# Two attention blocks: transposed exponentials moved within SBUF, value products 512 queries wide, shares of a step rearranged

## The chip, the cores and the metric

The kernel runs on one core of one Trainium2 chip. The metric is the device time of one execution in microseconds. The kernel before takes 3504.99 us, the median of three runs (3502.89 to 3509.22).

## The reference

Two layers follow each other on `x` of shape (4, 32, 32, 768) in fp32. Each is `x + attention(group_norm(x))`, with 32 groups of 24 channels and 12 heads of 64.

```
qkv = x @ Wqkv                       # second layer: + bias
scores = scale * q k^T + rel_h[..., :, None] + rel_w[..., None, :]
out = softmax(scores) @ v
x = x + out @ Wproj + bproj
```

`rel_h` and `rel_w` are products of each query with the table rows of its distance along height and width. An image has 1024 positions, so a head's scores are 1024 x 1024. The second layer has `scale` applied twice.

## The kernel before, in words

**Tiling.** There are 8 images (2 layers x 4), 6 pairs of heads in each, so 48 pairs `g`. A pair has 8 blocks of 128 queries, `n` = 0 to 7. One turn of the main loop (L566) is a unit (g, n), 384 in all. Channels lie on the partitions, and the two heads of a pair on partitions 0 to 63 and 64 to 127.

**What a unit does.** The order of all engines is written out by hand (`manual_schedule`, L566 to L625): an engine carries its instructions out in the order of the program, and one that waits holds those behind it. In unit (g, n):

- `biases` (L312) for the unit after the next: GpSimd adds the two position terms into `sc`.
- `scores` (L326) for the next unit: TensorE multiplies q and k into PSUM (tile `s`), VectorE subtracts from the biases and takes the row's extreme (L342), ScalarE exponentiates and sums (L346).
- `turn` (L358) for this unit: VectorE transposes the divided exponentials in 32 x 32 blocks into `tb` (L370).
- `divide` (L351) for the next unit: VectorE inverts the sums, GpSimd multiplies (L356).
- a share of the other matmuls, taken by `take` from the list `todo`.
- at n = 2 and n = 6 `weigh` (L386): the product of the transposed exponentials and v.

**Transposing through DRAM.** A 32 x 32 block transpose leaves the blocks themselves in place. Every second `turn` therefore writes `tb` of each head to DRAM (`td`, L373: 1 MB) and, one or two units later, reads it back as `pt` in 2 KB runs with the key's position spread over all partitions (`read_back`, L378). Both are issued by SyncE. A quarter is two blocks of queries; `weigh` takes two quarters, each with 256 query columns, and 8 key chunks for either head. The two heads use different columns of the TensorE array (128 x 64), while `scores`, the projections and `positions` split its rows (64 x 128) and the output projection uses the whole array.

**The shares.** One step of a generator in `todo` is a share: two half-array matmuls of 512 columns (`project_in` L202, tile `pj`), four of 256 columns (`project_values` L237, tile `pv`), or one full-array matmul of 512 columns (`project_out` L467, tile `o`). At n = 0 `todo` gets the q and k projections of the next pair (24 shares), half of two pairs' values (12) and a part of the output projection (12, in pairs that have one). The list `shares` (L570) says how many of the 48 go into each n; `first` (L608) says how many come ahead of `turn`, which orders VectorE's evictions against its transposes.

**Lists of later work.** Closures in `early` run at the start of the next unit, those in `later` one unit after that, those in `behind` and `behind2` after `scores` one or two units on. The q projection queues `positions` (L269, tile `tp`: products with the distance tables, written to DRAM by ScalarE's queue as `tdr`), and its second half queues `diagonals` (L295), 16 small DMAs on SyncE which read `rel` back for the next pair. SyncE's queue also carries the weights, the images, residuals and results.

**Buffers.** `pt` has two buffers for each head (8 KB a partition each), `tb` three (8 KB), `sc` six. PSUM holds two `s` tiles of two banks, and two tiles of two banks for all else.

Of the kernel before, what the change touches and what calls it, by code (L numbers as in the profile page):

```python
# [31 lines left out]
FP = mybir.dt.float32  # L32
# [4 lines left out]
P = 128  # L37
B, HW, C = 4, 32, 768
S = HW * HW
NH, D = 12, 64  # L40
NC = C // P
NT = S // P
# [3 lines left out]
HALF = 512  # L46
LAYERS = 2
NP = NH // 2
# [6 lines left out]
def attention_blocks(ctx: ExitStack, tc: tile.TileContext, a: dict, out: bass.AP):  # L55
    nc = tc.nc
# [8 lines left out]
    vpool = ctx.enter_context(tc.tile_pool(name="v", bufs=3))  # L65
    scpool = ctx.enter_context(tc.tile_pool(name="sc", bufs=6))
    tmppool = ctx.enter_context(tc.tile_pool(name="tmp", bufs=1))
    tbpool = ctx.enter_context(tc.tile_pool(name="tb", bufs=3))
    ptpool = ctx.enter_context(tc.tile_pool(name="pt", bufs=2))
    relpool = ctx.enter_context(tc.tile_pool(name="rel", bufs=2))  # L70
    iopool = ctx.enter_context(tc.tile_pool(name="io", bufs=4))
    small = ctx.enter_context(tc.tile_pool(name="small", bufs=4))
# [11 lines left out]
    NPAIR = NI * NP  # L84
# [117 lines left out]
    def project_in(g, which, i):  # L202

        im, pair = divmod(g, NP)
        xn, w = xn_of[im], w_of[g, which]
        cols = slice(i * HALF, (i + 1) * HALF)
        if i == 0:
            tag = "qk"[which]
            qk_of[g, which] = qkpool.tile([P, S], FP, tag=tag, name=f"{tag}_{g}")
        t = ps_m.tile([P, 2, HALF], FP, tag="m", name=f"pj_{g}_{which}_{i}")  # L210
        for c in range(NC):
            for a in range(2):
                rows = slice(a * D, (a + 1) * D)
                nc.tensor.matmul(  # L214
                    t[:, a, :], lhsT=w[rows, c, :], rhs=xn[c][rows, cols],
                    start=(c == 0), stop=(c == NC - 1),
                )
            if c < NC - 1:
                yield True
        to, t = qk_of[g, which], [t[:, a, :] for a in range(2)]  # L220
        if which == 1:
            to = to.rearrange("p (a m) -> p a m", a=4)[:, :, i * P : (i + 1) * P]
            t = [x.rearrange("p (m a) -> p a m", a=4) for x in t]
        else:
            to = to[:, cols]
        if images[im][0] == 0:
            nc.scalar.copy(to, t[0])  # L227
        else:
            nc.scalar.activation(to, t[0], AF.Identity, bias=bqkv[:, which, pair : pair + 1])
        nc.vector.tensor_tensor(to, t[1], to, ALU.add)  # L230
        if which == 0:
            (later if g else mid).append(lambda: positions(g, i))
        if i == 1 and g + 1 < NPAIR:
            later.append(lambda: load_w(g + 1, which))
        yield True
# [121 lines left out]

    def turn(g, n):  # L358

        quarter, j = divmod(n, 2)
        for h in range(2):
            if j == 0:
                tb_of[h] = tbpool.tile([P, HW, 2, HW], FP, tag="tb", name=f"tb_{g}_{n}_{h}")
            tb = tb_of[h]
            nc.vector.transpose(tb[:, :, j, :], sc_of[g, n, h])  # L370
            if j == 1:
                td = dram2.tile([P, S * 2], FP, tag=f"td{h}", name=f"td_{g}_{n}_{h}")
                nc.sync.dma_start(out=td, in_=tb.rearrange("p k n i -> p (k n i)"))  # L373
                (behind if quarter % 2 else behind2).append(
                    lambda queue=None, h=h, td=td: read_back(g, quarter, h, td, queue)
                )

    def read_back(g, quarter, h, td, queue=None):  # L378
        pt = ptpool.tile([P, 4, NT, 2 * HW], FP, tag=f"pt{h}", name=f"pt_{g}_{quarter}_{h}")
        pt_of[g, quarter, h] = pt  # L380
        (queue or nc.sync).dma_start(
            out=pt.rearrange("p r k t -> p r (k t)"),
            in_=td.rearrange("(r j) (a t) -> (j a) r t", r=4, a=4),
        )

    def weigh(g, quarters):  # L386

        if quarters[0] == 0:
            attn_of[g] = apool.tile([P, S], FP, tag="attn", name=f"attn_{g}")
        n = len(quarters)
        av = ps_m.tile([P, S], FP, tag="m", name=f"av_{g}_{quarters[0]}")[:, : n * 2 * P]
        for at, quarter in enumerate(quarters):
            for k in range(NT):
                for h in range(2):
                    rows = slice(h * D, (h + 1) * D)
                    nc.tensor.matmul(  # L399
                        av[rows, at * 2 * P : (at + 1) * 2 * P], lhsT=v_of[g][:, k, rows],  # L400
                        rhs=pt_of[g, quarter, h][:, :, k, :], start=(k == 0), stop=(k == NT - 1),
                    )
        at = quarters[0] * 2 * P
        to = attn_of[g][:, at : at + n * 2 * P].rearrange("p (q n r i) -> p q r n i", q=n, n=2, r=4)
        av = av.rearrange("p (q r n i) -> p q r n i", q=n, n=2, r=4)
        im, pair = divmod(g, NP)
        if images[im][0] == 0:
            nc.vector.tensor_copy(to, av)
        else:
            for q in range(n):  # L410
                nc.vector.tensor_scalar(to[:, q], av[:, q], bqkv[:, 2, pair : pair + 1], None, ALU.add)

    def cuts(im):
        return [0, NC // 2, NC] if im + 1 < NI else [0, NC // 2, NC - 1, NC]
# [86 lines left out]

    early, mid, later, behind, behind2 = [], [], [], [], []

    def run(todo):
        while todo:  # L510
            todo.pop(0)()
# [30 lines left out]
    with tc.manual_schedule(engines=ENGINES):  # L542
# [23 lines left out]
        for at, (g, n) in enumerate(units):  # L566
            im, pair = divmod(g, NP)
            end = im + 1 == NI
            if n == 0:
                shares = [6, 6, 0, 6, 12, 6, 0, 12]  # L570
                ins = (todo if at == 0 else []) + prepare(g + 1)
                if pair < 3:
                    if at == 0:
                        shares = [12, 6, 0, 6, 12, 6, 0, 0]
                    todo = ins + (put_out(im - 1, 1, range(4 * pair, 4 * pair + 4)) if im else [])
                elif pair < NP - 1:
                    todo = ins + put_out(im, 0, range(4 * pair - 12, 4 * pair - 8))
                    if pair == 3 and not end:
                        stages, apply = norm(im + 1)
                else:  # L580
                    todo = ins + put_out(im, 0, range(8, 12))
                    if end:
                        fetch_last()
                        todo += put_out(im, 1, range(12)) + put_out(im, 2, range(0, 12, 2))
                        shares = [6, 6, 0, 6, 6, 2, 0, 4]
            if (pair, n) in loads and not end:
                load_x(im + 1, loads[pair, n])
            if im + 1 < B:
                if (pair, n) in loads0:
                    load_x(im + 1, loads0[pair, n], loads0[pair, n] + AHEAD)  # L590
                if pair < 3 and n in (1, 3, 5, 6):
                    c, i = divmod(4 * pair + n // 2, 2)
                    x = xn_of[im + 1][c % AHEAD][:, i * HALF : (i + 1) * HALF]
                    later.append(lambda c=c, i=i, x=x: stats(im + 1, (c + AHEAD) % NC, i, x))
            run(early)
            early, later = later, early
            if at + 2 < len(units):
                biases(*units[at + 2])
            if at + 1 < len(units):
                scores(*units[at + 1])  # L600
            run(behind)
            behind, behind2 = behind2, behind
            if pair == 3 and n in stages and not end:
                stages[n]()
            if pair == 4 and n in (2, 4, 6) and not end:
                apply(n // 2 - 1)
            share = shares[n]
            first = 3 if n == NT - 1 else 2 if end and pair == NP - 1 and n in (3, 4) else 0  # L608
            first = min(first, share)
            take(todo, first)  # L610
            share -= first
            turn(g, n)
            if at + 1 < len(units):
                divide(*units[at + 1])
            if pair == 4 and n == 7 and not end:
                for chunks in ((3, 4), (5,)):
                    take(todo, 3)
                    share -= 3
                    for c in chunks:
                        apply(c)  # L620
            take(todo, share)
            if n == 6:
                weigh(g, (0, 1))
            elif n == 2 and g:
                weigh(g - 1, (2, 3))  # L625
        for read in behind:
            read(nc.scalar)
        take(todo, 12)
        for quarter in (2, 3):
            weigh(NPAIR - 1, (quarter,))  # L630
        todo = put_out(NI - 1, 2, range(1, 12, 2))
        take(todo, len(todo))

# [54 lines left out]
```

## Time and profile before

| | before |
|---|---|
| median of three runs | 3504.99 us |
| span of the profiled execution | 3507.0 us |
| mean granted TensorE clock | 0.998 |
| idle of TensorE | 44.7 us, 25.7 of it at the start |
| DMA | 1084.54 MB, mean 309 GB/s |
| td<-tb, SyncE | x384, 1024 KB, 5.9 us to landing |
| pt<-td, SyncE | x382, 1024 KB, 7.6 us to landing |
| rel<-tdr, SyncE | x760, 32 KB, 2.3 us to landing |

The profile is of one execution, and of it the page gives the span alone. The chain of work that ended last is followed back from the last instruction; where it stays on one engine, that engine's own work sets the time. In its list in order of time a line has start, length, engine, tile, source line and the number of instructions. Idle time of an engine off the chain costs nothing.

### The profile page before, as it was taken

Reading aid. Unit: us, or ns where it says so; the run is one execution under the profiler, and the core shown is the slowest. Engines: PE = TensorE matmul, PEld = TensorE weight load, DVE = VectorE, ACT = ScalarE, POOL = GpSimd, SP = SyncE. Lnnn points to the kernel's source line nnn. Section 1 sums busy time; section 2 is a strip of 40 time slices with the busy share of each in tenths; the row PEclk is TensorE's granted clock in tenths of the full one; section 3 lists DMA queues with packets and bytes.
Section 4 is the critical chain, followed back from the end, with each engine's and each line's share of the span. In section 5 each row is a group of like instructions: output and inputs, shape, how many; then the busy total and the mean of one; then the engine's idle time right before and its main releaser. Section 6 shows DMA issues by size and latency. Waiting matters only on the chain.

```text
span 3507.0 us, 55102 instructions
## 1 busy us (share of the span) xinstructions
PE 3462.3 (99%) x21120; PEld 1921.4 (55%) x21120; DVE 2381.1 (68%) x3676; ACT 1227.5 (35%) x2040; POOL 2729.9 (78%) x1546
## 2 busy tenths in 40 slices
PE   6999999999999999999999999999999999999999
PEld 4555555555555555555555555555555555555554
DVE  4666767767677676767767667666666667666666
ACT  2334333333333333333333333333333333333331
POOL 3888887778777787788777788787787778787774
PEclk9999999999999999999999999999999999999999
DMA  4889989999899898898989989899889988898877
GB/s 137 312 308 311 332 293 337 319 316 326 304 329 323 313 316 313 312 324 305 326 305 326 320 292 332 311 331 306 300 327 324 321 298 316 319 322 295 311 275 281
DMA packets 624857, 1084.54 MB, mean 309 GB/s; under 512 B 247120, under 2 KB 310096, under 8 KB 575440
## 3 DMA queue, kind: packets, MB, share of 16 engines
q1 hardware_dynamic: 569008, 1028.29, 83.4%
q10 hardware_dynamic: 55584, 52.72, 4.4%
q8 instruction: 166, 2.72, 0.3%
q14 instruction: 99, 0.81, 0.1%
HBM read 580.59 MB, written 500.27 MB: 308 GB/s over the span
## 4 chain that ended last, share of the span: by engine, by line
PE 97%; DMA 2%; DVE 0%; SPq 0%; issue 0%; ACT 0%; POOL 0%; ACTq 0%; DVEq 0%
PE pj L214 28%; PE s L333 19%; PE av L399 19%; PE o L475 14%; PE pv L249 14%; PE tp L281 3%; DMA tdr<-t 1%; DMA pt<-td 1%; SPq L307 0%; DMA td<-tb 0%; DMA wo<-in_wo 0%; DMA xn<-in_x 0%; DVE st L152 0%; DMA rel<-tdr 0%; DMA per<-mv 0%
## 5 line engine op out<-in xcount | busy, mean ns | idle before, releaser
L319 POOL TENSOR_TENSOR sc<-rel 128x1024 f32<-128x1024 f32 x768 | 1890.4, 2485 | 38.2 <-DMA rel<-tdr 38.2
L356 POOL TENSOR_SCALAR sc<-sc,sm 128x1024 f32<-128x1024 f32 x768 | 855.1, 1127 | 686.1 <-DVE sm L353 669.2
L346 ACT ACTIVATE sc<-sc,sm 128x1024 f32<-128x1024 f32 x768 | 879.8, 1147 | 1370.9 <-DVE sm L342 1368.7
L342 DVE CUSTOM_DVE_ANT_0 sc<-s,sc 128x1024 f32<-128x1024 f32 x768 | 909.8, 1222 | 293.3 <-PE s L333 266.4
L214 PE MATMUL pj<-xn,w 64*128 64x512 f32 x4608 | 1033.5, 591 | 26.8 <-DVE xn L193 25.7
L370 DVE STREAM_TRANSPOSE tb<-sc 128x1024 f32<-128x1024 f32 x768 | 910.7, 1222 | 22.9 <-DMA td<-tb 20.5
L214 PEld LDWEIGHTS pj<-xn,w 64*128 64x128 f32 x4608 | 453.2, 188 | 568.6 <-issue 536.6
L333 PE MATMUL s<-k,q 64*128 64x512 f32 x3072 | 750.1, 598 | 7.0 <-DVE sm L342 6.9
L399 PE MATMUL av<-pt,v 128*64 128x256 f32 x6144 | 689.1, 382 | 6.1 <-DMA pt<-td 6.1
L399 PEld LDWEIGHTS av<-pt,v 128*64 128x64 f32 x6144 | 434.5, 137 | 289.8 <-ACT v L259 35.6
L249 PE MATMUL pv<-wv,xn 64*128 64x256 f32 x4608 | 515.7, 376 | 0.0
L249 PEld LDWEIGHTS pv<-wv,xn 64*128 64x128 f32 x4608 | 448.3, 187 | 90.8 <-issue 30.1
L475 PE MATMUL o<-attn,wo 128*128 128x512 f32 x1080 | 475.8, 597 | 0.2 <-DMA wo<-in_wo 0.2
L333 PEld LDWEIGHTS s<-k,q 64*128 64x128 f32 x3072 | 288.5, 187 | 299.5 <-issue 275.5
L475 PEld LDWEIGHTS o<-attn,wo 128*128 128x128 f32 x1080 | 201.4, 190 | 271.4 <-issue 260.9
L260 DVE TENSOR_TENSOR v<-pv,v 128x256 f32<-128x256 f32 x192 | 81.5, 425 | 277.6 <-ACT v L259 277.6
L259 ACT COPY v<-pv 128x256 f32<-128x256 f32 x192 | 71.5, 372 | 330.7 <-PE pv L249 282.9
L286 ACT COPY t<-tp 128x1024 f32<-128x1024 f32 x96 | 97.2, 1012 | 245.5 <-PE tp L281 148.5
L346 ACT ACTIVATION_READ_ACCUMULATOR sc<-sc,sm 128x1 f32 x768 | 143.6, 187 | 0.0
L230 DVE TENSOR_TENSOR q<-pj,q 128x512 f32<-128x512 f32 x96 | 66.4, 692 | 107.5 <-ACT q L227 56.0
L230 DVE TENSOR_TENSOR k<-pj,k 128x512 f32<-128x512 f32 x96 | 66.4, 692 | 95.5 <-ACT k L227 49.0
L281 PEld LDWEIGHTS tp<-tab,q 64*128 64x128 f32 x1536 | 100.0, 187 | 39.9 <-issue 39.6
(34 smaller groups left out, 787.6 us busy)
## 6 DMA issues: line engine op xcount, KB each, us to landing
td<-tb SPq DMA_DIRECT2D x384, 1024.0 KB, 5.9
pt<-td SPq DMA_DIRECT2D x382, 1024.0 KB, 7.6
tdr<-t ACTq DMA_DIRECT2D x96, 512.0 KB, 6.3
w<-in_wqk SPq DMA_DIRECT2D x96, 384.0 KB, 7.5
rel<-tdr SPq DMA_DIRECT2D x760, 32.0 KB, 2.3
part<-res SPq DMA_DIRECT2D x84, 256.0 KB, 5.5
res<-part SPq DMA_DIRECT2D x84, 256.0 KB, 9.1
wv<-in_wv SPq DMA_DIRECT2D x24, 768.0 KB, 8.7
```

The costliest lines, as they stand in the source:

```text
L214: nc.tensor.matmul(t[:, a, :], lhsT=w[rows, c, :], rhs=xn[c][rows, cols], start=(c == 0), stop=(c == NC - 1),)
L230: nc.vector.tensor_tensor(to, t[1], to, ALU.add)
L249: nc.tensor.matmul(t[:, a, k, :], lhsT=xn[c][rows, (2 * i + k) * P : (2 * i + k + 1) * P], rhs=w[rows, c, :], start=(c == 0), stop=(c == N ...
L281: nc.tensor.matmul(ps[:, h, j, :], lhsT=q[rows, at * P : (at + 1) * P], rhs=tabs[l][rows, :], start=True, stop=True,)
L319: nc.gpsimd.tensor_tensor(sc.rearrange("p (a k) (u l) -> p a (k u) l", a=4, l=8), rel[:, h, 0, n, :].unsqueeze(1).unsqueeze(3).to_broadcas ...
L333: nc.tensor.matmul(ps[h][:, cols], lhsT=q[rows, n * P : (n + 1) * P], rhs=k[rows, cols], start=True, stop=True,)
L342: nc.vector.tensor_tensor_reduce(out=sc, in0=ps[h], in1=sc, scale=-scale, scalar=BIG, op0=ALU.add, op1=ALU.min, accum_out=st[:, 0, h : h + 1],
L346: nc.scalar.activation(sc, sc, AF.Exp, bias=st[:, 0, h : h + 1], scale=-1.0, accum_out=st[:, 1, h : h + 1],)
L356: nc.gpsimd.tensor_scalar(sc, sc, st[:, 2, h : h + 1], 1.0, ALU.mult, ALU.mult)
L370: nc.vector.transpose(tb[:, :, j, :], sc_of[g, n, h])
L399: nc.tensor.matmul(av[rows, at * 2 * P : (at + 1) * 2 * P], lhsT=v_of[g][:, k, rows], rhs=pt_of[g, quarter, h][:, :, k, :], start=(k == 0) ...
L475: nc.tensor.matmul(t, lhsT=wo_of[im, o, c], rhs=attn_of[im * NP + c][:, cols], start=(c == c0), stop=(c == c1 - 1),)
```

## The change

The two heads of two blocks now share one tile `tb` of 16 KB a partition, with two buffers. When both blocks are in it, `move` issues 16 DMAs on SyncE from `tb` straight to `pt`, each from 32 partitions to every fourth of 128, in runs of 4 KB. `pt` holds four blocks of both heads (32 KB a partition) and has one buffer. `weigh` takes four blocks at once: 512 query columns a matmul, at n = 5 for the first half and at n = 1 of the next pair for the second. The list `behind2` goes; a move is issued in the unit after its second `turn`. The shares per n are rearranged, three of them precede `turn` at n = 6 as well as at n = 7, and `positions` of the first half of q runs one unit after its projection instead of two. After the last unit, all remaining shares come ahead of the last `weigh`. [...]

```diff
-    tbpool = ctx.enter_context(tc.tile_pool(name="tb", bufs=3))
-    ptpool = ctx.enter_context(tc.tile_pool(name="pt", bufs=2))
+    tbpool = ctx.enter_context(tc.tile_pool(name="tb", bufs=2))
+    ptpool = ctx.enter_context(tc.tile_pool(name="pt", bufs=1))
...
-            (later if g else mid).append(lambda: positions(g, i))
+            (mid if not g else later if i else early).append(lambda: positions(g, i))
...
     def turn(g, n):
-        quarter, j = divmod(n, 2)
+        b, j = divmod(n, 2)
+        if j == 0:
+            tb_of[b] = tbpool.tile([P, HW, 2, 2, HW], FP, tag="tb", name=f"tb_{g}_{b}")
+        tb = tb_of[b]
         for h in range(2):
...
-            nc.vector.transpose(tb[:, :, j, :], sc_of[g, n, h])
-            if j == 1:
-                td = dram2.tile([P, S * 2], FP, tag=f"td{h}", name=f"td_{g}_{n}_{h}")
-                nc.sync.dma_start(out=td, in_=tb.rearrange("p k n i -> p (k n i)"))
-                (behind if quarter % 2 else behind2).append(
-                    lambda queue=None, h=h, td=td: read_back(g, quarter, h, td, queue)
+            nc.vector.transpose(tb[:, :, h, j, :], sc_of[g, n, h])
+        if j == 1:
+            behind.append(lambda: move(g, b, tb))
+
+    def move(g, b, tb):
+        half, u = divmod(b, 2)
+        if u == 0:
+            pt_of[g, half] = ptpool.tile(
+                [P, 2, 4, NT * 4 * HW], FP, tag="pt", name=f"pt_{g}_{half}"
+            )
+        pt = pt_of[g, half].rearrange("(j a) u r x -> a j u r x", a=4)
+        src = tb.rearrange("p (a k) h n i -> p a (k h n i)", a=4)
+        for a in range(4):
+            for r in (0, 2, 1, 3):
+                nc.sync.dma_start(out=pt[a][:, u, r, :], in_=src[r * HW : (r + 1) * HW, a, :])
+
+    def weigh(g, half):
...
+        av = ps_m.tile([P, S], FP, tag="m", name=f"av_{g}_{half}")[:, :HALF]
+        pt = pt_of[g, half].rearrange("p u r (k h x) -> p (u r) k h x", k=NT, h=2)
+        for k in range(NT):
+            for h in range(2):
+                rows = slice(h * D, (h + 1) * D)
+                nc.tensor.matmul(
+                    av[rows, :], lhsT=v_of[g][:, k, rows], rhs=pt[:, :, k, h, :],
+                    start=(k == 0), stop=(k == NT - 1),
                 )
...
-                shares = [6, 6, 0, 6, 12, 6, 0, 12]
+                shares = [12, 0, 6, 6, 12, 0, 6, 6]
...
-                        shares = [12, 6, 0, 6, 12, 6, 0, 0]
+                        shares = [12, 6, 6, 6, 12, 0, 0, 0]
...
-                        shares = [6, 6, 0, 6, 6, 2, 0, 4]
+                        shares = [6, 0, 6, 5, 4, 0, 5, 2]
...
-            first = 3 if n == NT - 1 else 2 if end and pair == NP - 1 and n in (3, 4) else 0
+            first = 0 if n < 6 else 2 if end and pair == NP - 1 else 3
...
-            if n == 6:
-                weigh(g, (0, 1))
-            elif n == 2 and g:
-                weigh(g - 1, (2, 3))
-        for read in behind:
-            read(nc.scalar)
-        take(todo, 12)
-        for quarter in (2, 3):
-            weigh(NPAIR - 1, (quarter,))
+            if n == 5:
+                weigh(g, 0)
+            elif n == 1 and g:
+                weigh(g - 1, 1)
+        run(behind)
+        take(todo, len(todo) * NC)
+        weigh(NPAIR - 1, 1)
...
-    nc = bacc.Bacc("TRN2", target_bir_lowering=False, num_devices=1)
+    nc = bacc.Bacc("TRN2", target_bir_lowering=False, num_devices=1, dynamic_dma_scratch_size=1024)
```

More of the change, by code (lines that the diff above doesn't have):

```diff
@@ L358, in turn @@
     def turn(g, n):
-        quarter, j = divmod(n, 2)
+        b, j = divmod(n, 2)
+        if j == 0:
+            tb_of[b] = tbpool.tile([P, HW, 2, 2, HW], FP, tag="tb", name=f"tb_{g}_{b}")
+        tb = tb_of[b]
         for h in range(2):
-            if j == 0:
-                tb_of[h] = tbpool.tile([P, HW, 2, HW], FP, tag="tb", name=f"tb_{g}_{n}_{h}")
-            tb = tb_of[h]
-            nc.vector.transpose(tb[:, :, j, :], sc_of[g, n, h])
-            if j == 1:
-                td = dram2.tile([P, S * 2], FP, tag=f"td{h}", name=f"td_{g}_{n}_{h}")
-                nc.sync.dma_start(out=td, in_=tb.rearrange("p k n i -> p (k n i)"))
-                (behind if quarter % 2 else behind2).append(
-                    lambda queue=None, h=h, td=td: read_back(g, quarter, h, td, queue)
-                )
@@ L378, in read_back @@
[L378 to L405, printed above, removed]
@@ new lines, in weigh @@
+    def weigh(g, half):
+        if half == 0:
+            attn_of[g] = apool.tile([P, S], FP, tag="attn", name=f"attn_{g}")
+        av = ps_m.tile([P, S], FP, tag="m", name=f"av_{g}_{half}")[:, :HALF]
[6 more added lines that the diff above has]
+                    start=(k == 0), stop=(k == NT - 1),
+                )
+        to = attn_of[g][:, half * HALF : (half + 1) * HALF]
+        to = to.rearrange("p (q n r i) -> p q r n i", q=2, n=2, r=4)
+        av = av.rearrange("p (q r n i) -> p q r n i", q=2, n=2, r=4)
@@ L409, in weigh @@
         else:
-            for q in range(n):
+            for q in range(2):
                 nc.vector.tensor_scalar(to[:, q], av[:, q], bqkv[:, 2, pair : pair + 1], None, ALU.add)
@@ L501, in project_out @@
         yield True
-    early, mid, later, behind, behind2 = [], [], [], [], []
+    early, mid, later, behind = [], [], [], []
     def run(todo):
@@ L601, in attention_blocks @@
             run(behind)
-            behind, behind2 = behind2, behind
             if pair == 3 and n in stages and not end:
```

## The prediction

> **What bounds the kernel now.** I read the page's busy shares and its chain first, then the chain in order of time for one pair, then the groups of the DMA issues, and last SyncE's queue beside VectorE.
>
> ```profile
> PE 3462.3 (99%) x21120; PEld 1921.4 (55%) x21120; DVE 2381.1 (68%) x3676; ACT 1227.5 (35%) x2040; POOL 2729.9 (78%) x1546
> PE 97%; DMA 2%; DVE 0%; SPq 0%; issue 0%; ACT 0%; POOL 0%; ACTq 0%; DVEq 0%
> ```
>
> TensorE is busy 3462.3 of 3507.0 us and carries 97% of the chain; DMA carries 2%. Of the idle 44.7 us, 25.7 are the wait for the first normalised image. The page's DMA row stands at 8 to 9 tenths, yet between 210 and 3420 us TensorE is busy 3208.55 of 3210.00 us. So halving the bytes is worth nothing by itself there. Only what changes TensorE's own sequence, or makes it wait, moves the time. The sequence, from the chain in order of time (start, length, line, passes; each fp32 matmul of the program runs as two passes):
>
> ```profile
> 1532.92 1.72 PE s L333 x8
> 1534.64 7.06 PE av L399 x64
> 1541.69 1.92 PE s L333 x8
> 1543.61 10.50 PE o L475 x24
> 1554.11 1.92 PE s L333 x8
> 1556.03 5.15 PE pj L214 x24
> 1561.18 1.72 PE s L333 x8
> 1562.89 5.15 PE pj L214 x24
> 1568.04 0.89 PE tp L281 x16
> 1568.94 1.72 PE s L333 x8
> 1570.65 7.06 PE av L399 x64
> 1577.71 1.09 PE tp L281 x16
> ...
> 1615.31 10.50 PE o L475 x24
> ```
>
> A pair lasts 1615.31 - 1543.61 = 71.70 us. A 512-column pass on a half array takes 5.15 / 24 = 214.6 ns, so two side by side 429.2; twelve full-array passes elsewhere take 5.35 against 10.50 for 24, so one pass is (10.50 - 5.35) / 12 = 429.2 ns and the rest, 0.20 us, is paid once per group. Likewise `s` takes 1.72 after a row-split group and 1.92 after `o` or `av`; `tp` 0.89 and 1.09. Each visit to `o` therefore costs 0.20 on entry and 0.20 on leaving, 0.40 us, besides its passes.
>
> [...] Here 429.2 per side-by-side pair of 512 columns, and for `pv` at 256 columns 5.18 / 24 = 215.8; twice that less 429.2 is 2.4 ns. [...] No operation before shows an SBUF to SBUF transfer[...].
>
> **The change, part by part.**
>
> *Value products, 512 wide.* 6144 passes become 3072. Pass work: 64 x 215.8 / 2 = 6.91 us per weighing before (7.06 with its entry), 32 x 214.6 = 6.87 after. 0.04 x 96 weighings = 3.8 us gained. Bounds: 0 if the loss is per column, 5.5 if the 0.15 entry goes too. The 3072 weight loads removed (137 ns each, 421 us of PEld) lie beside running matmuls: in `av`, PEld is idle 290 us. Worth nothing.
>
> *Shares.* Of 48 shares per pair, 36 are projections and the last 12 the output projection. Before, [6, 6, 0, 6, 12, 6, 0, 12] leaves exactly the final 12 for n = 7: one visit to `o`. After, [12, 0, 6, 6, 12, 0, 6, 6] spends 36 by n = 4, so `o` runs in n = 6 and in n = 7, with unit 0's `s` of the next step between: s, o, s, o, s. One visit more per pair, 0.40 us. Pairs 3 to 46 have 12 such shares: 44 x 0.40 = 17.6 us lost. Bounds: 8.8 if only entry counts, 17.6 if both. I take 17.6, since both steps stand in the chain above. Visits to `av` stay two per pair, in n = 5 and n = 1 instead of 6 and 2. The last pair keeps its six visits.
>
> *DMAs.* Per pair 8 + 8 transfers of 1 MB go, 64 of 128 KB come. Issue and landing, from the answers by line:
>
> ```profile
> L373 SPq DMA_DIRECT2D td<-tb x384: 319/332/1607, 80.4 to 3474.9; - x192
> L307 SPq DMA_DIRECT2D rel<-tdr x760: 302/449/1812, 50.6 to 3389.6; - x190
> ```
>
> The three figures are the least, median and greatest ns on SyncE. 64 x 0.33 = 21 us of SyncE per pair replace 8 x 0.33 + 8 x 0.38 = 5.7; with the 16 `rel` DMAs (7.2) and some 10 us of others that is 40 of 72. SyncE is not full, so only its order matters. A move needs 16 x 0.33 = 5.3 us to issue and some 2 us for the last to land: 7.3 us. [...] I take 9.
>
> *Are the moves in time?* VectorE's transposes end 6.5 us after their unit's `s` starts (`s` at 1507.11, transposes 1511.26 to 1513.62). A unit of 6 shares lasts 1.72 + 5.15 = 6.87 us, so `turn` of n = 3 ends as unit 4 starts. Unit 4 has 12 shares (12.05 us), unit 5 only `s` (1.72) before `weigh`: 13.8 us of cover, less what stands ahead on SyncE. Ahead stand the 16 `rel` DMAs. `positions` of the second half now runs at n = 2 instead of 3; after TensorE's 0.9, ACT's 1.0 and the transfer's 6.3 median they can go at about the start of unit 3, take 7.2 to 10.7, and leave SyncE 1 to 4 us into unit 4. So 10 to 13 us remain for 9 needed. The other half: unit 0 has 12 shares, unit 1 `tp` and `s`, 14.9 us; ahead stand two `res` writes which wait for VectorE's eviction of the last `o` group, about 2 us in. 12.5 us remain. Both fit: cost 0. Without cover each microsecond late costs 48 us a half. Behind the waiting move stand only weight and image loads due units later.
>
> *One `pt` buffer, two `tb`.* The first move of a half waits for the weighing before it; `weigh` ends with unit 5 (or 1), the move follows in unit 6 (or 2) and is due 3 units later. Each `tb` is read a unit and more before its rewrite. Cost 0; the queue behind is as above. VectorE's three `xn` normalisations after n = 7 of pair 4 (4.4 us) lose 5 us of their long unit; by their lengths they end some 0.4 us before the sixth projection step needs them. Seven times at most 2 us; I take 0.
>
> *Evictions and PSUM.* The same in number and in the alternation of two buffers; hidden under the groups as before. GpSimd's 7.2 us a unit against 6.87 to 7.3 us in the shortest: no change.
>
> *Ends.* In the last 88 us TensorE waits 0.22 + 0.20 + 2.40 + 0.58 us; 14 shares (12 us) now precede the last weighing and cover a 9 us move, but its two evictions of 0.48 are both waited for: gain 2 (from -3 to 3). At the start, 57 to 210 us, TensorE is idle 9.2 us and some passes run at the half clock; the first read-back stood behind `rel` in SyncE's queue and a move lands sooner than write and read. Gain 2, from -6 to 8.
>
> Sum: 17.6 - 3.8 - 2 - 2 = +9.8 us. The sum is a difference, made on the profiled execution (span 3507.0; what lies around it isn't shown); the three timed runs lie at 3502.89 to 3509.22 about it, so I add it to the median: 3504.99 + 9.8 = 3514.8.
>
> **Rivals.**
> A, moves late. For it: SyncE is in order, `rel` stands ahead[...]; against: of 1084 MB some 403 go, so the DMA load falls from 88% (the queues' shares added) to some 55%. At 1 us late in each half +96, at 2 us in one half +96: 3525 to 3620. Waits between the 16 DMAs themselves, if overlapping writes are assumed in their interleaved partitions, would be one more way in: four rounds of 2.4 us, 10 us.
> B, not slower: the start. If the earlier first weighing lets TensorE avoid all its 9.2 us of waits and 4 us of half clock there (the mean clock of that stretch is 0.97 of 153 us), and the tail gains 3, then 13.8 - 13 - 3 = -2, 3503. It decides from 14 us of recovered waits; there are about 16 in all, so at best -0.1% unless a mode change costs less than shown (8.8 instead of 17.6: -11, 3494).
> C, the added visit costs nothing[...]: 3505 less 3.8 and the ends, 3497 to 3505. [...]
>
> **How the numbers follow.** A difference under 0.2%, 7 us, is about what a measurement of this kernel can't tell from none. My forecast has 0.58, with 3508 to 3520 of its own: of that 0.11 lies under 3512, 0.47 over. A has 0.28, all slower. B and C have 0.14: 0.05 faster, 0.09 within. So 0.05, 0.20, 0.75. The range runs from 3502 (leaves out half of B and C) to 3575 (leaves out the upper third of A).
>
> **What would show it.** Right: in the chain a pair of 72.0 us with two groups of 12 `o` passes, each 5.35 and followed by an `s` of 1.92; `av` x32 of about 7.0; no `av` wait on pt after the first pair; DMA near half busy. Wrong: TensorE or its loads waiting for the moved tile where `weigh` starts in n = 5 or 1 (A); pairs still 71.7 (C); a first 210 us shorter by over 8 (B).

## The result, and the profile after

The changed kernel takes 3996.14 us (median of four runs, 3993.51 to 4001.39) beside 3506.7 us (four runs, 3502.89 to 3509.22) for the kernel before: a ratio of 1.140, with an interval of 1.138 to 1.141. The forecast of 3514.8 had the direction, and a small part of the size.

The spans of the profiled executions are 3507.0 and 3999.5 us, so there are 492.5 us to find. First two lines of the page before and then three of the page after: busy time of the engines, one DMA queue's share (packets, MB, share of the 16 engines), and the group of the value products (count, then busy us and mean ns, then idle before it and what ended most of that).

```profile
q1 hardware_dynamic: 569008, 1028.29, 83.4%
L399 PE MATMUL av<-pt,v 128*64 128x256 f32 x6144 | 689.1, 382 | 6.1 <-DMA pt<-td 6.1
...
PE 3622.1 (91%) x18048; PEld 1757.0 (44%) x18048; DVE 2380.1 (60%) x3676; ACT 1225.7 (31%) x2040; POOL 2715.2 (68%) x1546
q1 hardware_dynamic: 459472, 627.88, 58.0%
L391 PE MATMUL av<-pt,v 128*64 128x512 f32 x3072 | 815.2, 691 | 322.2 <-DMA pt<-tb 198.3
```

TensorE is busy 91% of the span and no longer 99%. The DMA engines are less loaded than before (58.0% against 83.4% on this queue), and of TensorE's idle time, now 377.4 us, 322.2 stand in one place: ahead of `av`, most of it waiting for the moved tile `pt`. The chain on the page after can be followed back through about 1% of the span only, so a pair is read from TensorE's timeline instead: start, length, line, passes, and in brackets the idle time before and what ended it.

```profile
1776.34 1.88 PE L333 MATMUL s<-k,q 64*128 64x512 f32 x8
1782.43 8.74 PE L391 MATMUL av<-pt,v 128*64 128x512 f32 x32 [4.21 <-DMA pt<-tb]
1791.11 1.99 PE L333 MATMUL s<-k,q 64*128 64x512 f32 x8
1793.02 5.42 PE L464 MATMUL o<-attn,wo 128*128 128x512 f32 x12
1798.37 1.99 PE L333 MATMUL s<-k,q 64*128 64x512 f32 x8
1800.29 5.42 PE L464 MATMUL o<-attn,wo 128*128 128x512 f32 x12
...
1821.47 7.09 PE L391 MATMUL av<-pt,v 128*64 128x512 f32 x32 [0.94 <-DMA pt<-tb]
```

The two `o` groups of 12 passes are there as foretold. The weighing at n = 5 waits 4.21 us and then takes 8.74 instead of 7.09: its first passes are slow, and the trace's clock record grants one half from 1782.39 on for 3.41 us. Over all 48 pairs the n = 5 weighing waits 214.4 us (4.5 on average), the other 107.8 us. 66 of the 96 weighings take 7.8 to 9.5 us from the start of the first pass to that of the last, where an undisturbed one takes 6.5: 134.4 us more in sum. The mean granted clock is 0.954 (before 0.998). Waits of 322.2, less 6.1 that the kernel before had ahead of `av`, and 134.4 of slow passes make 450.5 of the 492.5 us. The added visits to `o`, less the gain of the wider products, are another 44 x 0.3 = 13. The remaining 29 us are spread over many places and were not traced one by one.

Now SyncE's queue in the same stretch (start, length, line, transfer, count):

```profile
1749.63 11.52 SPq L380 DMA_DIRECT2D pt<-tb  x16
1761.25 7.99 SPq L307 DMA_DIRECT2D rel<-tdr  x16
1769.34 10.67 SPq L380 DMA_DIRECT2D pt<-tb  x16
```

and the issues of line 380 (least, median and greatest ns of one; then issue to landing):

```profile
L380 SPq DMA_DIRECT2D pt<-tb x3072: 469/594/3342, 85.3 to 3977.3; - x192
DMA to landing us min/median/max: 2.4/2.7/7.1
```

The DMAs of a move take 0.594 us each on SyncE, not 0.33. With the gaps a move's 16 stand 0.64 apart and occupy the queue for 10.7 us. From the weighing at n = 1, whose end lets the first move go (`pt` has one buffer), SyncE works without a pause until 1780.01, and the last piece has landed when `av` begins 2.4 us later: 32.8 us. TensorE has 28.6 us of work in that time (1749.63 to 1778.22). The difference is the 4.2 us wait. The median over the pairs is the same: 32.7 us from the end of the weighing to the landing of the second move, 28.6 us of work.

The waits at n = 1 have another cause. Apart from the last pair they are 4.9 to 6.5 us in 17 pairs, most of them among the first three of an image, and at most 1.2 us in the others. One such place in the timeline of all engines (ACTq is ScalarE's queue):

```profile
2608.01 16.15 SPq L380 DMA_DIRECT2D pt<-tb  x16
2620.73 0.37 ACTq L288 DMA_DIRECT2D tdr<-t  x1
2626.70 5.99 PE L391 MATMUL av<-pt,v 128*64 128x512 f32 x14 [5.34 <-DVE sm L353]
```

and SyncE's waits in 2600 to 2630 us (line, what it waited for, us, times, longest):

```profile
SPq L380 <- DMA tdr<-t: 5.0, 1, 5.0
```

A move has nothing to do with `tdr`, the products with the distance tables that ScalarE's queue writes to DRAM. But the trace's records of the 4605 DMA instructions name a completion counter for each, and both queues draw from the same eight, in turn (from one DMA of SyncE to the next the counter goes on by one 4392 times, and by two 103 times):

```
queue line tile      issued   landed   counter  waits for counter
SP    L380 pt<-tb    2616.79  2620.02  101      101
SP    L380 pt<-tb    2618.04  2620.70  102      102
ACT   L288 tdr<-t    2620.73  2623.67  104      -
SP    L380 pt<-tb    2623.69  2626.29  104      104
```

The move's last DMA drew the same counter as the `tdr` write, as the next after it, so it waited for that write to land, and ScalarE issued the write only in the next unit. The move took 16.15 us of the queue in place of 10.7, and TensorE stood for 5.34 us. The label of that wait names VectorE's `sm`, but that was done at 2626.19, and the moved tile landed later, at 2626.29. The same records for the whole run find one of the last two DMAs of a move held by a `tdr` write in 17 pairs. They are the 17 pairs with the waits of 4.9 to 6.5 us, 92.4 of the 107.8 us, and in each of them `av` begins 0.1 to 0.5 us after the landing. Another 11.5 us stand in the last pair.

### The profile page after: what moved, and what is told of

Its sections match the earlier page's. It is cut to its first block, busy times and chain, and to the rows that moved or that the text cites. A ratio compares the mean times of both kernels' runs of the same rounds, so it can differ in the third digit from the quotient of the medians.

```text
span 3999.5 us, 51680 instructions
## 1 busy us (share of the span) xinstructions
PE 3622.1 (91%) x18048; PEld 1757.0 (44%) x18048; DVE 2380.1 (60%) x3676; ACT 1225.7 (31%) x2040; POOL 2715.2 (68%) x1546
## 5 line engine op out<-in xcount | busy, mean ns | idle before, releaser
L391 PE MATMUL av<-pt,v 128*64 128x512 f32 x3072 | 815.2, 691 | 322.2 <-DMA pt<-tb 198.3
L391 PEld LDWEIGHTS av<-pt,v 128*64 128x64 f32 x3072 | 268.9, 159 | 861.6 <-issue 776.1
L249 PE MATMUL pv<-wv,xn 64*128 64x256 f32 x4608 | 506.3, 377 | 0.0
L464 PE MATMUL o<-attn,wo 128*128 128x512 f32 x1080 | 487.6, 601 | 0.0
L400 DVE COPY attn<-av 128x512 f32<-128x512 f32 x48 | 33.2, 692 | 362.5 <-PE av L391 362.5
L403 DVE TENSOR_SCALAR attn<-av,bqkv 128x256 f32<-128x256 f32 x96 | 42.1, 480 | 314.9 <-PE av L391 314.9
```

The costliest lines, as they stand in the source:

```text
L249: nc.tensor.matmul(t[:, a, k, :], lhsT=xn[c][rows, (2 * i + k) * P : (2 * i + k + 1) * P], rhs=w[rows, c, :], start=(c == 0), stop=(c == N ...
L391: nc.tensor.matmul(av[rows, :], lhsT=v_of[g][:, k, rows], rhs=pt[:, :, k, h, :], start=(k == 0), stop=(k == NT - 1),)
L464: nc.tensor.matmul(t, lhsT=wo_of[im, o, c], rhs=attn_of[im * NP + c][:, cols], start=(c == c0), stop=(c == c1 - 1),)
```

## The experiments

Theory 1: SyncE's issue time and the order move, `rel`, move make the n = 5 wait. Theory 2: shared counters make the n = 1 wait. Rivals: the 32 neighbouring partitions that a DMA reads bound the move (the author's assumption, "ports" in the expectations); the added `o` visits cost far more than 0.4 us.

### rel behind the second move (e1)

```diff
-            later.append(lambda: diagonals(g))
+            wait = lambda: later.append(lambda: behind.append(lambda: diagonals(g)))
+            later.append(wait if g else lambda: diagonals(g))
```

> The changed kernel with the 16 rel DMAs of a pair issued in unit 4 behind the second move instead of in unit 3 ahead of it. Theory 'SyncE's loop' (weighing ends, move of 11.5 us, rel 8.0, move of 10.7, landing 2.4, next weighing; 32.8 us where TensorE needs 28.3): the wait before the first half's weighing falls from a mean of 4.5 us to under 0.7, and with it the passes at the lower clock after it (8.2 to 9.4 us instead of 6.5 a weighing); the second half stays as it is; 3996 - 48 x (4.5 + 1.7) = about 3700 us, 3660 to 3760. Rival 'the move alone is too long': the wait stays over 3 us, 3900 to 4000 us.

3869.89 us (one run). The waits at n = 5 fall from 214.4 to 0.1 us: SyncE's loop, shortened by the 8 us of `rel`, fits (from the weighing's end to the landing 27.2 us, with 28.6 of work). The time misses what was expected, because the other wait grows from 107.8 to 244.5 us. SyncE's waits:

```profile
SPq L381 <- DMA tdr<-t: 220.9, 43, 9.1
```

Shifting 16 DMAs shifted which of the move's DMAs draws a counter after a `tdr` write: now one of the last four does so in 39 pairs, and these are, the last pair apart, the 39 whose n = 1 weighing waits 5.0 us or more.

### Source spread over all partitions (e2)

```diff
-        src = tb.rearrange("p (a k) h n i -> p a (k h n i)", a=4)
+        src = tb.rearrange("(j r) (a k) h n i -> r j a (k h n i)", r=4, a=4)
...
-                nc.sync.dma_start(out=pt[a][:, u, r, :], in_=src[r * HW : (r + 1) * HW, a, :])
+                nc.sync.dma_start(out=pt[a][:, u, r, :], in_=src[r][:, a, :])
```

> The changed kernel, each of the 16 DMAs of a move reading every fourth partition (32 of 128) instead of 32 in a row; count, size and destination stay. It reads other rows, so the output is not the reference's. Theory 'ports'[...]: the pitch of the DMAs falls from 0.64 us to 0.33 to 0.45, a move from 10.7 us to under 7.5, and the time to 3520 to 3620 us. Theory 'issue' (SyncE takes 0.59 us for such a DMA, whatever it touches): pitch 0.64, 3970 to 4020 us.

3920.1 us (one run), 76 less, and between the two ranges expected. The issues of line 380:

```profile
L380 SPq DMA_DIRECT2D pt<-tb x3072: 458/592/2404, 87.9 to 3898.4; - x192
DMA to landing us min/median/max: 1.9/2.1/6.4
```

The queue's share of the DMA engines falls from 58.0 to 45.6% and the landing from 2.7 to 2.1 us, so 32 neighbouring partitions do cost something. But the issue stays at 0.592: which partitions are read doesn't set the pace. The n = 5 wait falls from 4.5 to 3.5 us, about the shorter landing.

### Eight DMAs of 256 KB a move (e3)

```diff
-            for r in (0, 2, 1, 3):
-                nc.sync.dma_start(out=pt[a][:, u, r, :], in_=src[r * HW : (r + 1) * HW, a, :])
+            for r in (0, 2):
+                nc.sync.dma_start(
+                    out=pt[a][:, u, r : r + 2, :],
+                    in_=src[(r + a % 2) * HW : (r + a % 2 + 1) * HW, a // 2 * 2 : a // 2 * 2 + 2, :],
+                )
```

> The changed kernel with a move made of 8 DMAs of 32 partitions x 8 KB instead of 16 of 4 KB: the same bytes from the same 32 partitions in a row, half the issues. The pieces land in other places, so the output is not the reference's. Theory 'ports': 1.2 to 1.3 us a DMA, a move still 10 to 11 us, 3950 to 4020 us. Theory 'issue': 0.6 to 0.65 us a DMA, a move 5.2 us, first-half waits under 0.7 us, 3520 to 3650 us.

3717.4 us (one run), 279 less, again between the two ranges expected.

```profile
L380 SPq DMA_DIRECT2D pt<-tb x1536: 469/850/3064, 86.1 to 3692.7; - x192
DMA to landing us min/median/max: 3.3/4.7/8.9
```

The median of 0.85 is not the price of one DMA of twice the bytes. By their place in the move, the first two DMAs take 0.48 and 0.59 us (medians of 192 moves), just as in the changed kernel, where all that follow take 0.59 to 0.60. Here those that follow take 0.63 to 1.36, and each lands 4.7 instead of 2.7 us after its issue. So twice the bytes don't lengthen the first two issues; what holds the later ones is not shown. A move's issues take 7.5 us instead of 10.7, which is a higher rate from the same partitions: they don't bound the changed kernel. The n = 5 wait is 2.5 us on average, the n = 1 wait 0.2.

### Before, with the output projection in two visits (e4)

```diff
-                shares = [6, 6, 0, 6, 12, 6, 0, 12]
+                shares = [6, 6, 0, 6, 12, 6, 6, 6]
```

> The kernel before, with only the last 12 shares of a pair split 6 and 6 over n = 6 and n = 7 (shares [6, 6, 0, 6, 12, 6, 6, 6]); in n = 6 the o groups come after turn and ahead of the weighing. Theory 'mode changes' of the prediction: 0.40 us for a second visit to o; here one side of it touches av instead of s (s, o, av, s, o, s), which saves 0.20 to 0.25 of leaving: 44 x 0.15 to 0.40 = 7 to 18 us slower, 3512 to 3524 us. Rival: a visit costs nothing in the time, 3503 to 3509 us.

3698.07 us, ratio 1.0555 (1.0532 to 1.0579): a miss, and not a price for the visit. The timeline of all engines near n = 6:

```profile
1701.80 5.42 PE L475 MATMUL o<-attn,wo 128*128 128x512 f32 x12
...
1711.26 1.25 DVE L370 STREAM_TRANSPOSE tb<-sc 128x1024 f32<-128x1024 f32 x1 [5.71 <-DMA td<-tb]
1712.43 0.12 DVE L353 RECIPROCAL sm<-sm 128x2 f32<-128x2 f32 x1
1712.47 1.39 DVE L486 SCALAR_TENSOR_TENSOR res<-o,bo,res 128x512 f32<-128x512 f32 x2
...
1713.25 3.25 PE L399 MATMUL av<-pt,v 128*64 128x256 f32 x14 [6.03 <-DVE res L486]
```

VectorE's transpose waits 5.71 us for a `tb` buffer that a DRAM write still reads (203.2 us of such waits in the whole run, 20.5 in the kernel before), the eviction of `o` stands behind it, and `av` waits for the PSUM tile. The list of shares changes the order of VectorE's queue, not only TensorE's modes. The `o` group itself is 5.42, as long as it is in the changed kernel.

### rel behind, and tdr written by SyncE (e5); tdr alone (e6)

```diff
-        nc.scalar.dma_start(
+        nc.sync.dma_start(
             out=td[i * HALF : (i + 1) * HALF, :].rearrange("(j p) r -> p j r", p=P),
```

With e1's edit it is e5, without it e6. Then the write stands in SyncE's own queue, so a move can't wait for a `tdr` write that is not yet issued.

> As e1 (rel behind the second move), and the two tdr writes of a pair issued by SyncE instead of ScalarE, so that every DMA after the first pair stands in one queue. Theory 'shared counters': the DMAs of both queues take eight completion counters in turn, and one waits until the DMA eight before it has landed; the last one or two DMAs of a move have drawn the counter after a tdr write that ScalarE issues only in the next unit, and so wait for it with SyncE's queue behind them (the second half's 5.1 us in e1). Then both halves' waits vanish, pairs of 72.0 us, 3507 + 14 + ends = 3510 to 3535 us. Rival 'the second half is late by its own transfers': it keeps waits of 3 us and more, 3700 to 3870 us.

> The changed kernel with the two tdr writes on SyncE and nothing else moved. Theory 'shared counters': the second half's waits (107.8 us and the slow passes after them, some 155 in all) go, the first half keeps about 4.5 us a pair, or somewhat more since tdr now stands in the queue ahead of rel: 3800 to 3880 us. Rival: the second half's waits stay, 3950 to 4020 us.

e5: 3598.63 us, ratio 1.0262 (1.0245 to 1.0279). 398 of some 490 us are gone. The n = 5 waits are 0.7 us in sum, those at n = 1 41.1, and SyncE's waits for `tdr` (220.9 us ahead of the moves in e1) are no longer among its nine longest, the least of which is 13.4 us in sum. Pairs without a disturbance last 72.0 us from one q projection to the next, exactly what the prediction gave for a pair. The expected 3510 to 3535 was too low: of the 84.8 us that its span has over 3507.0, 17.4 lie after the last pair's q projection. Of the rest, 13 are for the added visits, some 29 in six pairs where the image changes (74.8 to 79.5 us instead of 72.0), 8 in pairs 2 and 3, and the other 17 are spread.

e6: 4004.26 us (one run), where 3800 to 3880 was expected. The n = 1 waits fall from 107.8 to 27.7 us, as theory 2 says. But those at n = 5 rise from 214.4 to 327.5. SyncE's and TensorE's waits tell why:

```profile
SPq L288 <- ACT t L286: 505.0, 73, 20.9
```

```profile
PE av L391 <- DMA pt<-tb: 344.5, 57, 8.5
```

The `tdr` writes now stand in SyncE's queue ahead of the first move and wait there for ScalarE's copy of `t`. The move starts 3.3 us after the weighing and no longer at once, and the second one lands 35.2 us after it, where TensorE has 28.6 us of work. Both edits are needed together; each alone adds to the wait of the other weighing.

### Steps of before (e7), and positions put back (e9)

e7 is e5 with the shares, the `first` rule and the weighing places (n = 6 and 2) of before:

```diff
-                shares = [12, 0, 6, 6, 12, 0, 6, 6]
+                shares = [6, 6, 0, 6, 12, 6, 0, 12]
...
-            first = 0 if n < 6 else 2 if end and pair == NP - 1 else 3
+            first = 3 if n == NT - 1 else 2 if end and pair == NP - 1 and n in (3, 4) else 0
...
-            if n == 5:
+            if n == 6:
                 weigh(g, 0)
-            elif n == 1 and g:
+            elif n == 2 and g:
                 weigh(g - 1, 1)
```

e9 is e7 with `positions` of the first half of q two units after its projection, as before:

```diff
-            (mid if not g else later if i else early).append(lambda: positions(g, i))
+            (later if g else mid).append(lambda: positions(g, i))
```

> As e5, with the shares and the places of weigh of the kernel before (shares [6, 6, 0, 6, 12, 6, 0, 12], weigh at n = 2 and n = 6): the moves within SBUF and the 512-column products alone. A move now has 15 to 20 us until its weighing, and o is visited once a pair. Theory: no waits, pairs of 71.70 - 0.08 = 71.6 us; 3507 - 4 and 0 to 4 at the ends: 3496 to 3508 us. Rival 'one pt buffer': the first move of a half waits for the weighing before it and pushes rel and the second move on, so that GpSimd's biases or the weighing are late: 3550 us and more.

> As e7, with positions of the first half of q back in the list later (two units after its projection, as in the kernel before). In e7 tp stands right behind the q projection that it reads and waits 0.70 + 0.70 us for its eviction, 73.3 us a pair. Theory: that wait goes, pairs of 71.6 us, 3600 - 45 x 1.7 = about 3524 us, 3515 to 3535; what stays over the kernel before is the last pair. Rival: GpSimd, which in e7 waits for rel (behind the second move), or the moves become the next wait: pairs of 72.5 us and more, over 3550 us.

e7: 3600.41 us, ratio 1.0271 (1.0255 to 1.0286), a miss. TensorE waits for `pt` only 11.4 us in the whole span, yet each pair lasts 73.3 us. The chain of e7 in order of time:

```profile
1811.99 5.17 PE pj L214 x24
1817.16 0.02 issue
1817.19 0.70 ACT q L229
1817.88 0.02 issue
1817.91 0.70 DVE q L230
1818.61 0.04 issue
1818.65 1.16 PE tp L281 x16
```

One unit after the projection, `tp` comes straight behind it and waits for the two steps that evict q, 1.4 us. In the changed kernel 12 shares in n = 0 stand between; with the old shares the early `positions` is a new wait in nearly every pair (`tp` waits for q 47 times, 73.6 us in all).

e9: 3532.2 us, ratio 1.0076 (1.0062 to 1.009), as expected. A pair without a disturbance is 71.6 us, 0.1 shorter than before (71.7): the wider products, and nothing lost. SyncE and TensorE in one pair (all engines' timeline):

```profile
1725.84 7.09 PE L392 MATMUL av<-pt,v 128*64 128x512 f32 x32
...
1732.97 11.60 SPq L381 DMA_DIRECT2D pt<-tb  x16
...
1745.93 10.61 SPq L381 DMA_DIRECT2D pt<-tb  x16
1756.64 9.59 SPq L308 DMA_DIRECT2D rel<-tdr  x16
1761.48 7.09 PE L392 MATMUL av<-pt,v 128*64 128x512 f32 x32
```

The moves are as slow as ever, 11.6 and 10.6 us, but the second leaves the queue at 1756.5 and is due at 1761.5.

### Moves on two queues (e8)

```diff
-                nc.sync.dma_start(out=pt[a][:, u, r, :], in_=src[r * HW : (r + 1) * HW, a, :])
+                (nc.scalar if a % 2 else nc.sync).dma_start(out=pt[a][:, u, r, :], in_=src[r * HW : (r + 1) * HW, a, :])
```

> The changed kernel with the 16 DMAs of a move dealt alternately to SyncE (a = 0, 2) and ScalarE (a = 1, 3). Theory 'issue time of a queue': 8 DMAs of 0.64 us on each side by side, a move takes 5.3 us, the first half's waits fall below 1 us, 3550 to 3750 us, what stays being ScalarE's exponentials held behind the waiting DMAs. Rival[...]: the two queues together still need 10 to 11 us a move, 3900 us and more.

3843.2 us (one run), between the two ranges expected.

```profile
L380 SPq DMA_DIRECT2D pt<-tb x1536: 469/593/2877, 85.0 to 3813.7; - x192
L380 ACTq DMA_DIRECT2D pt<-tb x1536: 477/606/1987, 89.6 to 3816.8; - x192
```

Two queues issue at the same 0.6 us each as one does alone, so the time belongs to the queue. The waits for `pt` fall (1.5 us at n = 5, 0.3 at n = 1), and ScalarE pays:

```profile
ACT v L259 <- DMA pt<-tb: 197.7, 35, 7.0
ACT sc L346 <- DMA pt<-tb: 175.8, 32, 7.3
ACT q L229 <- DMA pt<-tb: 130.0, 24, 6.4
```

While ScalarE waits to issue, its exponentials and copies stand behind the move.

### What is left: the end (e10) and the start (e12)

e10 is e9 with the last pair's second half moved from two queues, and its weighing done in two parts of 256 queries. In the diff `us` is (0,) and then (1,):

```diff
+                queue = nc.scalar if a % 2 and g == NPAIR - 1 and half else nc.sync
+                queue.dma_start(out=pt[a][:, u, r, :], in_=src[r * HW : (r + 1) * HW, a, :])
...
-        weigh(NPAIR - 1, 1)
+        for u in range(2):
+            weigh(NPAIR - 1, 1, (u,))
```

e12 is e10 with the same for the second move of pairs 0 to 2:

```diff
+                split = half and (g == NPAIR - 1 or g < 3 and u)
+                queue = nc.scalar if a % 2 and split else nc.sync
```

> As e9, and for the last pair: its last two moves dealt to SyncE and ScalarE (which has no exponentials left), and its last weighing in two halves of 256 queries, the first of which needs only the first move. Theory: the 10 us that TensorE waits in the last pair go, 3500 to 3512 us, within 0.2% of the kernel before or a little faster (pairs of 71.6 instead of 71.7). Rival: the wait lies with the first weighing of the last pair or with the queue, over 3518 us.

> The previous run with one edit: in pairs 0, 1 and 2, the second move of the second half also goes from two queues, eight DMAs from SyncE and eight from ScalarE. What is left of the loss in the previous run (span 3519.5 against 3507.0) lies, by the periods of its pairs, in pairs 1 to 4 (+10 us) and in small disturbances afterwards. In pairs 0 to 2 no output projection runs in n = 7, so the interval from one weighing to the next is about 26 us there, against 24 us for two moves and a landing and another move's worth for what else SyncE carries; TensorE waits 5.0, 2.0 and 5.5 us for the moved tile, and the weighing after a wait takes 8.2 to 9.2 us instead of 6.5. My theory, SyncE's issue time is what remains: halving the issue of that move takes about 5 us off each of the three, so the waits fall to 0 to 2 us in all and the passes run at full speed: some 12 + 6 us less, a span of about 3502 to 3506 and a ratio of 0.9990 to 1.0020. Rival, ScalarE pays for it: its exponentials stand behind eight issues of 0.6 us in n = 0, TensorE waits for VectorE or ScalarE instead, and the time stays at 3515 to 3525.

e10: 3522.08 us, ratio 1.0052 (1.0038 to 1.0066). The stretch after the last pair's q projection falls from 168.5 to 159.2 us (before: 158.8), so the end was got back; 3500 to 3512 was still a miss, because the start had been left out of the expectation. Before the projection of pair 5 e10 is 9.9 us behind the kernel before. There `av` waits 13.0 us up to 346 us, against 3.7 in the kernel before: pairs 0 to 2 have no output projection to cover the moves.

e12: 3523.13 us, ratio 1.0048 (1.0034 to 1.0062), no different from e10. TensorE's waits from 26 to 346 us:

```profile
PE pj L214 <- DVE xn L193: 25.4, 1, 25.4
PE s L334 <- DVE sm L343: 6.9, 6, 1.4
PE tp L281 <- DVE q L230: 6.8, 3, 2.6
...
PE av L395 <- ACT t L286: 0.2, 1, 0.2
```

The waits ahead of `av` are gone from this stretch (13.0 us in e10). In their place `tp` waits 6.8 us for q, whose copy on ScalarE waits for the moves' DMAs in three places, 13.6 us in all (nowhere in e10). TensorE's passes in the stretch also take 305.0 us instead of 298.9, at a mean clock of 0.96 instead of 0.97. The rival expectation holds: the time did not change, and half of the wait has another owner.

### Before, with av beside o (e11)

```diff
-                shares = [6, 6, 0, 6, 12, 6, 0, 12]
+                shares = [6, 6, 0, 6, 6, 6, 6, 12]
...
+            if n == 7 and not last:
+                weigh(g, (0, 1))
...
-            if n == 6:
+            if n == 6 and last:
```

In the other pairs no share precedes `turn` at n = 7 any more (three did). The last pair is left as it was, and so is its `first`.

> The kernel before with its DRAM path, the first weighing of a pair moved from n = 6 to n = 7 right ahead of the output projection, and shares [6, 6, 0, 6, 6, 6, 6, 12], so that no unit is left with scores alone. s, av, o, s has one change of array mode less than s, av, s, o, s. Theory 'mode changes', 0.20 us each: 44 x 0.2 = 9 us faster, 3494 to 3502 us. Rival: with shorter units in a row the transfers through DRAM (88% of the DMA engines' time) come late and TensorE or VectorE waits: 3520 us and more.

3528.18 us, ratio 1.007 (1.0056 to 1.0084): not the gain expected, but the rival's range. Undisturbed pairs do last 71.5 us instead of 71.7: one mode change fewer is 0.2 us, the step that the prediction read. But about half of the pairs are disturbed, 71.7 to 77.5 us. VectorE's wait for `tb` in e11, and below it in the kernel before:

```profile
DVE tb L370 <- DMA td<-tb: 199.6, 54, 7.6
...
DVE tb L370 <- DMA td<-tb: 20.5, 18, 6.5
```

As in e4, another order of shares and transposes brings VectorE to `tb` before the DRAM write has left it. No version was faster than the kernel before.

## Why the prediction was wrong

- *What bounds the kernel; bytes are worth nothing by themselves.* Right. The queue's share of the DMA engines fell from 83.4 to 58.0% and the time rose.
- *Value products, 3.8 us gained.* About right. e9's undisturbed pair is 0.1 us shorter than before, 0.08 was said.
- *The added visit, 0.40 us a pair.* Right as far as the runs show it. The pair of 72.0 us stands in e5 where nothing waits; e9, with one visit and the same value products, has 71.6. e11 shows one mode change fewer at 0.2. That is about 13 of 492 us.
- *A move: 16 x 0.33 + 2 = 7.3, "I take 9".* **The failed term.** An issue within SBUF takes 0.594 us, with gaps 0.64; a move is 10.7 us to issue and 12.8 to its last landing, and the four moves of a pair take 64 x 0.64 = 41 us of SyncE, not 21 (the terms of "40 of 72" make 38). The price was that of a 1 MB write to DRAM (0.33), not of this kind, and the step from 7.3 to 9 was the author's estimate, with no transfer within SBUF in the traces of before to rest on. It came short of 12.8, and it wasn't carried into the sum of the queue. Which partitions are read does not set the pace, as e2 (0.592 us an issue) and e3 (7.5 us a move) show. The waits between the 16 DMAs themselves that rival A left room for are not in the trace: they are issued 0.64 us apart, though each lands 2.7 us after its issue.
- *In time: 10 to 13 us of cover at n = 5, 12.5 at n = 1, cost 0.* **The step that failed.** The prediction put `rel` ahead of the second move and had it leave 1 to 4 us into unit 4, near the truth (5 us after its start in the stretch shown). It didn't put the first move ahead of `rel`, though it had named that move's wait for the weighing at n = 1 (one `pt` buffer, "Cost 0"). The loop is weighing, move, `rel`, move, landing: 11.5 + 8.0 + 10.7 + 2.4 and small gaps, 32.8 us against 28.6. A cover counted for the last link alone was 8.9 us, not 10 to 13, against 13.1 needed. e1, which takes `rel` out of the loop, ends that wait: 0.1 us is left of 214.4.
- *Behind the waiting move stand only loads due units later.* Too short. `rel` and the next move stood behind, and a move itself could stand behind ScalarE's `tdr` write, which the prediction did not name. e1, e5 and e6 show that: taking `tdr` off ScalarE's queue ends 80 of the 107.8 us in e6, and 203 of e1's 244.5 in e5.
- *One microsecond late costs 48 us a half* (rival A). Rival A, given 0.28, is what came; its rule is right, and the range drawn from it, to 3620, too narrow. Mean waits of 4.5 and 2.25 us make 324 by that rule. It left out the half clock after a wait, 134 us more: weighings of 6.5 us take 7.8 to 9.5 after waits of 3.3 us and more, and one took 8.2 after a wait of 2.2 us, all 66 with a clock of one half. The 30 others waited 1.2 us at most and took 6.5.
- *Ends: 2 us gained at each.* Wrong. The tail lost 23.6 us (182.4 against 158.8 from the last q projection on): the last pair has 6 shares in n = 0, not 12, and its n = 1 weighing waits 9.3 us. At the start the changed kernel is 63.7 us late by the q projection of pair 5, most of it the waits above and the slow passes after them; e10, which is rid of most of those, is still 9.9 late there.
- *The `xn` normalisations: at most 2 us, seven times, taken as 0.* Within that bound: TensorE waits for them 4.4 us in seven places.
- *Rival B and C* (start recovered, visit free) find no support in any run.

What stays open: why the issue of one of these DMAs takes 0.594 us, where a 1 MB write to DRAM took 0.332. Both e3's DMAs and the changed kernel's have 32 pieces, of 8 KB and of 4, and no run changes their number. Nor was a second buffer of `pt` tried, which would let the first move begin before the weighing ends; whether that alone would end the n = 5 wait is not shown.

## What to carry to other kernels

When a release and a due time are joined by one in-order queue, add up everything that the queue issues between the two events, each DMA at its own measured price, and compare that sum with the consumer's work in the same interval; cover counted from the last link alone hides the rest. A late input to a busy TensorE cost more here than its wait: 134 us of slower passes after it, on 322 of waits. Before giving a step to another queue or unit, list what the engine that carries the queue must do behind it: in e6, e8 and e12 a wait went from one owner to another, and in e4 and e11 another order of shares made a new one.

## What the runs showed of the hardware

- A DMA of 128 KB within SBUF (32 partitions, 4 KB runs) took 0.594 us of the issuing queue in the median, and 0.48 as the first of a move, while 1 MB writes to DRAM took 0.332. In the second place of a move one of 128 KB and one of 256 KB both took 0.59 (changed kernel and e3). Issued from two queues they took 0.593 and 0.606 (e8). For one DMA the issue is 0.6 of the 2.7 us to landing; for a move of 16 in one queue it is 10.7 of 12.8, most of it.
- In this program the 4605 DMAs of SyncE and ScalarE use eight completion counters, 575 or 576 times each, and 3391 of them carry a wait for their own counter. None of the 3391 starts before all DMAs that drew this counter earlier have landed, from whichever queue they come. A write that the other queue had not yet issued held a move for 5.0 us.
- TensorE's clock records of the changed kernel hold 70 stretches at one half, 369 us in all; the kernel before has 5, 17 us. 66 of the 70 fall on the 66 slow weighings. The mean clock falls from 0.998 to 0.954.
- Reading from every fourth partition instead of 32 neighbouring ones took the queue's share of the DMA engines from 58.0 to 45.6% and the landing from 2.7 to 2.1 us, and left the issue at 0.592.
- An instruction that waits held those behind it in the order of the program: VectorE's eviction of `o` stood behind a transpose that waited 5.71 us (e4), and ScalarE's copy of q behind the DMAs of moves for 13.6 us in three places (e12).
